# A two-layer perceiver on one core: which engine reads a score's PSUM bank first, and where the second-last chunk's last product and sum stand

## The chip, the cores and the metric

The kernel runs on one core of one Trainium2 chip. The metric is the device time of one execution in microseconds (us); lower is better. Three executions of the kernel before took 2023.55, 2024.21 and 2026.40 us, a median of 2024.21 us.

## The reference

Sixteen batches of 64 latent vectors (width 128) pass through two layers. Each layer has a cross attention to a long context, a sequence model and a feed-forward stage, each added to its input. Cut to what matters here:

```python
x = x + xattn0(ctx, norm(x))          # ctx: 16 batches of 1601 rows of 128
x = x + scan0(norm(x));  x = x + moe0(norm(x))
x = x + xattn1(ctx, norm(x), mask)    # the second layer's scores are masked
x = x + scan1(norm(x));  x = x + ffn1(x)   # ffn1 quantises its inputs to 4 bits

def xattn(ctx, lat):                  # 16 heads of 64
    s = q(lat) @ k(concat(ctx, lat)).T          # + mask
    return softmax(s) @ v(concat(ctx, lat)) @ Wo
```

All arithmetic is in float32 but for a bfloat16 intermediate in the quantiser.

## The kernel before, in words

**Attention groups.** The attention of a layer is cut into 32 groups: 16 batches times two halves of the heads. Both layers make 64 groups. A group takes 13 steps (`NT`); step i works on the i-th 128 rows of the context. The weights are folded in advance, so that a score needs one product of the query side with the transposed context, and the average one product with the context itself.

**A step.** `scores` makes a score tile `s` of 128x512 on TensorE (two matmul records, line 651) in one of three PSUM banks (pool `pss`, 3 buffers). ScalarE copies the tile to SBUF as `st` (line 658; in the second layer line 656, which adds the mask). VectorE keeps a running maximum `R` over the group's tiles, which reads the same bank (line 665, masked 663). The first tile of a group has no maximum, and the second one's reads the first's copy `st`. Once both readers are through, the bank goes to the score three steps on.

**Later steps.** When a group's 13 tiles are done, `maximum` (lines 674 to 685) reduces `R`, `spread` (692) spreads it over the partitions, and `weigh` subtracts it from `st`, two tiles at a time on VectorE (700), followed by the exponential on ScalarE (701). `average` (713) multiplies the weights with the context, 21 steps (`LAG`) behind the score; `gather` (722) takes the sums out of PSUM on VectorE. For the very last group `finish` (737 to 753) does this and normalises and transposes at once; `output` (785) then applies the output weights and adds to the latents `X` (789).

**Work in between.** Loading, normalising and transposing the context, the queries and the second and third parts of each layer are generators. `run` advances them a little after each step under a budget; a generator's `yield` of a tuple puts off its next piece by as many steps (`HOP` is two). For the last part of the second layer the tokens are cut into eight chunks of 128, which are worked off in pairs (0 and 1, 2 and 3, 4 and 5) and then singly (6, 7). Chunk 6's `scan1` and `ffn` are worked off beside the last groups. Chunk 7 holds the last batches and can only begin when the last group is finished: its `scan1` and `ffn` run alone at the end. In `ffn`, line 1393 copies the transposed hidden values `fh`, lines 1398 and 1399 multiply them with the down weights into `fo`, line 1400 adds `fo` to `X` and line 1401 stores the chunk. `layernorm` takes moments (144, 145, 155), a reciprocal root on GpSimd (135) and scales in `scaled` (162). `fill` (128, 130) issues matmuls whose result nobody reads, to keep TensorE running.

**What sets the order.** Each engine works through its own instructions in a fixed order. It is drawn up at compile time: a list scheduler takes, for each engine, the instruction traced earliest of those that are ready by its own estimate of durations. The kernel steers it with edges without a semaphore (`later`, `behind`): `behind` keeps what it traces behind the score evictions that `scores` has listed in `self.place`. Semaphores are added wherever two engines touch the same data or the same PSUM bank.

Of the kernel before, what the change touches and what calls it, by code (L numbers as in the profile page):

```python
# [36 lines left out]
AF = mybir.ActivationFunctionType  # L37
ALU = mybir.AluOpType
# [5 lines left out]
NB, L, D = 16, 64, 128  # L44
# [29 lines left out]
CG = 2  # L74
# [5 lines left out]
class Kernel:  # L80
# [78 lines left out]

    def scaled(self, eng, dst, src, mv, r, n):  # L160
        for c in range(n):
            eng.tensor_scalar(dst[:, c, :], src[:, c, :], mv[:, c, 0:1], r[:, c:c + 1], ALU.subtract, ALU.mult)

    def layernorm(self, dst, src, n, alone=False):

# [472 lines left out]
    def scores(self, g, i):  # L638

        nc, grp = self.nc, self.groups[g]  # L640
        lay, b, half = grp["key"]
        if i == 0:
            grp["st"] = []
            grp["R"] = self.at.tile([P, NQ], F32, tag="R", name=f"R{g}", bufs=2)
        if i % 2 == 0:
            n = min(2, NT - i)
            grp["st"].append(self.at.tile([P, n, NQ], F32, tag=f"st{n}", name=f"st{g}_{i // 2}", bufs=11 if n == 2 else 2))
        st, R = grp["st"][i // 2][:, i % 2, :], grp["R"]
        q = self.q_of[lay, b][:, half * 8:half * 8 + 8, :].rearrange("p h l -> p (h l)")
        s = self.pss.tile([P, NQ], F32, tag="s", name=f"s{g}_{i}")  # L650
        mm = nc.tensor.matmul(s, self.kv_of[lay, b][1][:, i * P:(i + 1) * P], q, start=True, stop=True)  # L651
        self.place["PE"].append(mm.ins)
        masked = lay == 1
        if masked:
            mc = self.mcol[:, i, b:b + 1]
            ev = nc.scalar.activation(st, s, AF.Identity, bias=mc)  # L656
        else:
            ev = nc.scalar.copy(st, s)  # L658
        self.place["ACT"].append(ev.ins)
        if i:  # L660
            last = grp["st"][0][:, 0, :] if i == 1 else R
            if masked:
                mx = nc.vector.scalar_tensor_tensor(R, s, mc, last, ALU.add, ALU.max)  # L663
            else:
                mx = nc.vector.tensor_tensor(R, s, last, ALU.max)  # L665
            self.place["DVE"].append(mx.ins)

    def maximum(self, g):

# [688 lines left out]
    def ffn(self, c0, CG):  # L1358
        nc, tc = self.nc, self.tc
        X = self.X[:, c0:c0 + CG, :]  # L1360
        TG = CG * P
        with tc.tile_pool(name="ff1", bufs=1) as one, tc.tile_pool(name="ff2", bufs=CG) as work:
            t1 = lambda shape, name: one.tile(shape, F32, tag=name, name="ff_" + name)
            xi, xT = t1([P, CG, D], "xi"), t1([P, TG], "xT")
            last = c0 + CG == C and CG == 1
            yield from self.layernorm(xi, X, CG, last)
            flat = xi.rearrange("p c d -> p (c d)")
            yield from self.quant(flat, flat, TG // 16, one, "qx")
            yield HOP
            self.transpose_tokens(xT, xi, CG, f"fft{c0}")  # L1370
            yield HOP
            hb = one.tile([P, CG, I4], F32, tag="hb", name=f"hb{c0}")
            for k in range(CG):
                tg, tu = self.tp(f"fg{k}"), self.tp(f"fu{k}")
                nc.tensor.matmul(tg[:, :I4], xT[:, k * P:(k + 1) * P], self.wgT, start=True, stop=True)  # L1375
                mm = nc.tensor.matmul(tu[:, :I4], xT[:, k * P:(k + 1) * P], self.wuT, start=True, stop=True)
                if c0 + CG == C and CG == 1:
                    self.fill(10, mm)
                sg, th = (work.tile([P, I4], F32, tag=x, name=f"f{x}{k}") for x in ("sg", "th"))
                yield from self.silu2(sg, tg[:, :I4], th)  # L1380
                nc.vector.scalar_tensor_tensor(hb[:, k, :], sg, 0.5, tu[:, :I4], ALU.mult, ALU.mult)
                yield 1.1
            flat = hb.rearrange("p c d -> p (c d)")
            yield from self.quant(flat, flat, CG * I4 // 16, one, "qh", ends=2 if last else 1)
            yield HOP
            hT = []
            for k in range(CG):
                hT.append(work.tile([IC, 512], F32, tag="hT", name=f"fh{c0}{k}"))
                for lo, hi in ((0, 2), (2, 4)) if last else ((0, 4),):
                    t = self.tp(f"ft{c0}{k}")  # L1390
                    for i in range(lo, hi):
                        nc.tensor.transpose(t[:IC, i * P:(i + 1) * P], hb[:, k, i * IC:(i + 1) * IC], self.ident)  # L1392
                    nc.scalar.copy(hT[k][:, lo * P:hi * P], t[:IC, lo * P:hi * P])
                yield 0.1
            yield HOP
            o = self.tp(f"fo{c0}")
            for k in range(CG):
                for i in range(4):
                    nc.tensor.matmul(o[:, k * D:(k + 1) * D], hT[k][:, i * P:(i + 1) * P], self.wdT[:, i, :], start=(i == 0), stop=(i == 3))  # L1399
            nc.vector.tensor_tensor(X, X, o[:, :CG * D].rearrange("p (c d) -> p c d", c=CG), ALU.add)  # L1400
            nc.sync.dma_start(out=self.out.rearrange("(c p) d -> p c d", p=P)[:, c0:c0 + CG, :], in_=X)
            yield 0.5


    def run(self, out):
# [3 lines left out]
        ng = len(self.groups)  # L1409
# [6 lines left out]
        between, prep = [], []  # L1416
# [26 lines left out]
                prep.append((start(lay, b) - 2 if lay or b else 12, 1, self.apart_scores(lay, b)))  # L1443
        prep.sort(key=lambda x: x[0])
        live = []
        n, go, budget, finished = 0, 0, 0.0, 0
        while n < (ng + 1) * NT + LAG + 8 or between:
            for lay in range(2):
                for b in range(NB):
                    if (lay or b > 1) and n == max(start(lay, b) - 48, 8):  # L1450
                        with self.behind():
                            self.context_load(lay, b)
                    if n == start(lay, b) + 14:
                        xeb = self.xeb_of[lay, b] = self.at.tile([P, D + 1], F32, tag="xeb", name=f"xeb{lay}_{b}", bufs=2)
                        self.nc.sync.dma_start(out=xeb, in_=self.xed[lay][b].partition_broadcast(P))
            while prep and prep[0][0] <= n:
                key, _, g = prep.pop(0)

                assert g.__name__ != "latents" or g.gi_frame.f_locals["lay"] == 0 or finished >= 3 + 2 * g.gi_frame.f_locals["gr"]
                live.append([n, g])  # L1460
            for x in list(live):
                if x[0] <= n:
                    try:
                        with self.behind(1):
                            r = next(x[1])
                        x[0] = n + r[0] if isinstance(r, tuple) else n
                    except StopIteration:
                        live.remove(x)
            if n >= 0:
                self.step(n, ng)  # L1470


                hold = ng * NT - 2 <= n < ng * NT + 4
                if n > ng * NT + LAG:
                    stages = [g for _, _, g in between]
                    tails = [chain(*stages[-2:])]
                    if len(stages) > 2:
                        tails.append(chain(*stages[:-2]))
                    while tails:
                        tails = [g for g in tails if self.trace(g, 1)]  # L1480
                    between = []
                if between and between[0][0] <= n:
                    budget = min(budget + between[0][1], 2.0)
                while budget > 0 and not hold and between and between[0][0] <= n and go <= n:
                    try:
                        with self.behind(1):
                            r = next(between[0][2])
                        if isinstance(r, tuple):
                            go = n + r[0]
                        else:  # L1490
                            budget -= r
                    except StopIteration:
                        between.pop(0)
                        finished += 1
            n += 1
# [42 lines left out]
    def step(self, n, ng):  # L1538
        g, i = divmod(n, NT)
# [3 lines left out]
        ga, ia = divmod(n - LAG, NT)  # L1543
        if 0 <= ga < ng and ia:
            if ia == 1:
                self.average(ga, 0)
            self.average(ga, ia)
            if ia == NT - 1:
                (self.finish if ga == ng - 1 else self.gather)(ga)

        for p in (g - 2, g - 1):
            o = n - (p + 1) * NT
# [82 lines left out]
```

## Time and profile before

| what | value |
|---|---|
| three executions, median (lowest to highest) | 2024.21 us (2023.55 to 2026.40) |
| the profiled execution's own time | 2023.47 us |
| its span in the profile | 2021.7 us |
| mean granted TensorE clock | 0.996 |
| busy: TensorE matmul, VectorE, ScalarE, GpSimd | 1974.8, 1563.8, 1382.3, 520.5 us |
| first layer, 0 to 1000 us: busy TensorE, VectorE, ScalarE | 973.99, 760.85, 756.31 us |
| second layer, 1000 to 1960 us: the same | 948.54, 766.88, 609.40 us |
| the end, 1960 to 2022 us: the same | 52.22, 36.03, 16.55 us |

The profile was taken in one execution of its own. Its span is what lies between the first and the last recorded instruction; 1.8 us of its time lie outside. In a row of the groups, the numbers after the first bar are the busy time in us and the mean of one in ns, and after the second bar the engine's idle time just before such an instruction and what ended most of it. In a row of the waits, the numbers are us in total, how often, and the longest. A matmul's end is modelled, so TensorE's busy time holds some waiting too.

### The profile page before, as it was taken

The numbers are of one execution on the slowest core, as the hardware profiler recorded it, in microseconds if no ns is written. First come the engines' busy times: TensorE is split into PE (matmuls) and PEld (weight loads), VectorE is DVE, ScalarE is ACT, GpSimd is POOL, SyncE is SP. The second block draws the span as 40 slices with busy tenths as digits, with TensorE's granted clock in tenths as the row PEclk, the third lists the DMA queues.
The fourth block names the chain that finished last, engine by engine and source line by source line (L and its number), as shares of the span: only waits on it lengthen the run. The fifth ranks groups of instructions, "written<-read, shape, count | busy, mean of one in ns | idle before, by whom it ended". The sixth has DMA issues, their size and how long they took to land. (4 is left out here: it accounts for less than half of the span.)

```text
span 2021.7 us, 32901 instructions
## 1 busy us (share of the span) xinstructions
PE 1974.8 (98%) x12123; PEld 1499.8 (74%) x12123; DVE 1563.8 (77%) x2954; ACT 1382.3 (68%) x2628; POOL 520.5 (26%) x579
## 2 busy tenths in 40 slices
PE   9999999999999989999999999999999999999998
PEld 6777777676777767778777787777778777787787
DVE  6977777886778887676988777898686979778884
ACT  5788878887768887566767657776565656666561
POOL 5111123542123442121543203542111121002000
PEclk9999999999999999999999999999999999999999
DMA  6111112321122321221221102221110110101000
GB/s 175 63 59 46 46 42 84 84 73 50 43 66 84 83 70 36 65 76 45 67 80 51 36 24 72 71 62 51 44 53 18 57 36 22 55 18 36 23 1 22
DMA packets 141805, 110.54 MB, mean 55 GB/s; under 512 B 11458, under 2 KB 127950, under 8 KB 141646
## 3 DMA queue, kind: packets, MB, share of 16 engines
q1 hardware_dynamic: 141102, 108.19, 18.5%
q8 instruction: 96, 1.57, 0.3%
q14 instruction: 63, 0.52, 0.1%
q10 hardware_dynamic: 544, 0.26, 0.0%
HBM read 79.97 MB, written 27.41 MB: 53 GB/s over the span
## 5 line engine op out<-in xcount | busy, mean ns | idle before, releaser
L713 PEld LDWEIGHTS av<-kv,st 128*128 128x128 f32 x6656 | 851.6, 192 | 317.3 <-issue 288.7
L713 PE MATMUL av<-kv,st 128*128 128x129 f32 x6656 | 868.1, 276 | 6.5 <-DVE aq L722 3.9
L651 PE MATMUL s<-qT,kvT 128*128 128x512 f32 x1664 | 853.0, 602 | 17.2 <-DVE R L665 14.2
L700 DVE TENSOR_TENSOR st<-st,mb 128x1024 f32<-128x1024 f32 (+1 forms) x448 | 501.7, 1132 | 1.3 <-PE mb L692 1.1
L701 ACT ACTIVATE st<-st 128x1024 f32<-128x1024 f32 (+1 forms) x448 | 444.9, 997 | 72.1 <-DVE st L700 68.8
L656 ACT ACTIVATE st<-s,mcol 128x512 f32<-128x512 f32 x416 | 283.5, 685 | 221.2 <-PE s L651 178.6
L658 ACT COPY st<-s 128x512 f32<-128x512 f32 x416 | 240.3, 581 | 130.4 <-PE s L651 103.1
L651 PEld LDWEIGHTS s<-qT,kvT 128*128 128x128 f32 x1664 | 259.6, 192 | 84.8 <-DVE R L665 36.1
L663 DVE SCALAR_TENSOR_TENSOR R<-s,mcol,R 128x512 f32<-128x512 f32 x352 | 262.0, 744 | 69.8 <-ACT st L656 68.4
L665 DVE TENSOR_TENSOR R<-s,R 128x512 f32<-128x512 f32 x352 | 240.9, 685 | 90.4 <-ACT st L658 89.3
L762 POOL TENSOR_TENSOR aq<-aq,rd 128x512 f32<-128x512 f32 x63 | 77.6, 1232 | 409.9 <-DVE rd L761 402.6
L565 POOL TENSOR_TENSOR kv<-kv,vec 128x384 f32<-128x384 f32 (+1 forms) x128 | 137.6, 1094 | 151.0 <-PE kt L625 71.7
L866 POOL TENSOR_TENSOR db<-sc_u,bb 128x512 f32<-128x512 f32 x64 | 84.7, 1326 | 134.4 <-DVE h L877 60.8
L883 POOL TENSOR_TENSOR sc_y<-sc_y,h 128x512 f32<-128x512 f32 x60 | 79.9, 1332 | 104.2 <-DVE h L882 80.0
L877 DVE TENSOR_TENSOR_SCAN h<-da,db 128x512 f32<-128x512 f32 x64 | 85.3, 1333 | 0.0
L616 ACT ACTIVATE kv<-kv,coff,crstd 128x128 f32<-128x128 f32 x182 | 76.5, 489 | 5.1 <-POOL coff L613 5.1
L665 DVE TENSOR_TENSOR R<-s,st 128x512 f32<-128x512 f32 x32 | 22.1, 689 | 72.3 <-ACT st L658 72.3
L607 ACT ACTIVATE scr<-kv,cmean 128x128 f32<-128x128 f32 x182 | 72.8, 400 | 6.9 <-DVE cmean L603 3.7
L722 DVE SCALAR_TENSOR_TENSOR aq<-xeb,ee,av 128x129 f32<-128x129 f32 x252 | 72.8, 341 | 1.4 <-PE av L713 1.3
L135 POOL TENSOR_TENSOR crstd<-cvar,neghalf 128x13 f32<-128x13 f32 x14 | 35.0, 2502 | 134.6 <-DVE cvar L611 134.4
L450 PE MATMUL q<-xnT,wqk 128*128 128x128 f32 x512 | 68.8, 277 | 0.0
L450 PEld LDWEIGHTS q<-xnT,wqk 128*128 128x128 f32 x512 | 62.9, 192 | 6.3 <-issue 3.1
(410 smaller groups left out, 1973.5 us busy)
## 6 DMA issues: line engine op xcount, KB each, us to landing
bb<-bcd SPq DMA_DIRECT2D x64, 256.0 KB, 4.4
xh<-kv SPq DMA_DIRECT2D x16, 832.0 KB, 4.8
kv<-xh SPq DMA_DIRECT2D x16, 832.0 KB, 5.5
kvT<-xhT SPq DMA_DIRECT2D x16, 800.0 KB, 4.5
xhT<-kvT SPq DMA_DIRECT2D x15, 800.0 KB, 3.4
kv<-in_ctx_dram SPq DMA_DIRECT2D x15, 768.0 KB, 5.5
ew<-in_e1T_dram SPq DMA_DIRECT2D x36, 64.0 KB, 1.9
ew<-in_e3T_dram SPq DMA_DIRECT2D x36, 64.0 KB, 1.9
```

The source lines that it names most:

```text
L450: nc.tensor.matmul(t[:, k * P:(k + 1) * P], self.wqk[:, g * 4 + k, :], xnT, start=True, stop=True)
L565: nc.gpsimd.tensor_tensor(kv[:, lo:hi, :D], kv[:, lo:hi, :D], self.row(self.vec[:, w1, :], [P, hi - lo, D]), ALU.mult)
L651: mm = nc.tensor.matmul(s, self.kv_of[lay, b][1][:, i * P:(i + 1) * P], q, start=True, stop=True)
L656: ev = nc.scalar.activation(st, s, AF.Identity, bias=mc)
L658: ev = nc.scalar.copy(st, s)
L663: mx = nc.vector.scalar_tensor_tensor(R, s, mc, last, ALU.add, ALU.max)
L665: mx = nc.vector.tensor_tensor(R, s, last, ALU.max)
L700: nc.vector.tensor_tensor(st, st, self.row(mb, [P, n, NQ]), ALU.subtract)
L701: nc.scalar.activation(st, st, AF.Exp)
L713: nc.tensor.matmul(o, st, self.kv_of[lay, b][0][:, i, :], start=(i == 0 and k % 2 == 0), stop=(i == NT - 1 and k % 2 == 1))
L866: nc.gpsimd.tensor_tensor(db, u, self.row(bb[:, 0, s % 2, :], both), ALU.mult)
L877: nc.vector.tensor_tensor_scan(flat(h), flat(da), flat(db), 0.0, ALU.mult, ALU.add)
```

## The change

It has two parts. In `scores`, the running maximum on VectorE is traced ahead of the copy on ScalarE. Both read the same bank, so the semaphore between them turns round: the copy now waits for the maximum of its own tile.

At the end, chunk 6's last product (`fo`) is traced ahead of `finish`: when the last average is traced, `upto_sums` advances the waiting generators until chunk 6's `ffn` has issued it. The sum into `X` (line 1400 before) and the store then come when the generator is next advanced; `later` gives the sum an edge behind the instruction that `scaled` last noted in `self.normed`. Chunk 7's `scan1` is advanced three pieces at once when the tail begins.

```diff
     def scaled(self, eng, dst, src, mv, r, n):
         for c in range(n):
-            eng.tensor_scalar(dst[:, c, :], src[:, c, :], mv[:, c, 0:1], r[:, c:c + 1], ALU.subtract, ALU.mult)
+            self.normed = eng.tensor_scalar(dst[:, c, :], src[:, c, :], mv[:, c, 0:1], r[:, c:c + 1], ALU.subtract, ALU.mult)
...
         masked = lay == 1
-        if masked:
-            mc = self.mcol[:, i, b:b + 1]
-            ev = nc.scalar.activation(st, s, AF.Identity, bias=mc)
-        else:
-            ev = nc.scalar.copy(st, s)
-        self.place["ACT"].append(ev.ins)
+        mc = self.mcol[:, i, b:b + 1] if masked else None
+
         if i:
...
             self.place["DVE"].append(mx.ins)
+        if masked:
+            ev = nc.scalar.activation(st, s, AF.Identity, bias=mc)
+        else:
+            ev = nc.scalar.copy(st, s)
+        self.place["ACT"].append(ev.ins)
...
-            nc.vector.tensor_tensor(X, X, o[:, :CG * D].rearrange("p (c d) -> p c d", c=CG), ALU.add)
+            alone = CG == 1 and not last
+            if alone:
+                self.summed = True
+                yield 0.0
+            x = nc.vector.tensor_tensor(X, X, o[:, :CG * D].rearrange("p (c d) -> p c d", c=CG), ALU.add)
+            if alone:
+                self.later(x, self.normed)
...
+        def upto_sums():
+
+            while not self.summed:
+                with self.behind(1):
+                    if next(between[0][2], None) is None:
+                        between.pop(0)
+
+        self.summed, self.upto_sums = False, upto_sums
...
                         tails.append(chain(*stages[:-2]))
+                    self.trace(tails[0], 3)
                     while tails:
...
             if ia == NT - 1:
-                (self.finish if ga == ng - 1 else self.gather)(ga)
+                if ga == ng - 1:
+                    self.upto_sums()
+                    self.finish(ga)
+                else:
+                    self.gather(ga)
```

## The prediction

> **What bounds the kernel now.** I read the page's busy times and groups first, then the waits by engine, then the timeline around the longest waits and around the end.
>
> ```profile
> PE 1974.8 (98%) x12123; PEld 1499.8 (74%) x12123; DVE 1563.8 (77%) x2954; ACT 1382.3 (68%) x2628; POOL 520.5 (26%) x579
> ...
> L651 PE MATMUL s<-qT,kvT 128*128 128x512 f32 x1664 | 853.0, 602 | 17.2 <-DVE R L665 14.2
> ...
> L658 ACT COPY st<-s 128x512 f32<-128x512 f32 x416 | 240.3, 581 | 130.4 <-PE s L651 103.1
> ...
> L665 DVE TENSOR_TENSOR R<-s,R 128x512 f32<-128x512 f32 x352 | 240.9, 685 | 90.4 <-ACT st L658 89.3
> ```
>
> TensorE is busy 98% of the span: it is the bound, and a change can only win what TensorE waits for. Its scores do wait, and what ends most of that is the running maximum R. The copy takes 581 ns, the maximum 685. The waits give totals:
>
> ```profile
> ACT st L656 <- PE s L651: 178.6, 186, 6.3
> DVE R L665 <- ACT st L658: 161.5, 125, 7.1
> DVE R L663 <- ACT st L656: 121.5, 111, 5.1
> ...
> PE s L651 <- DVE R L665: 14.2, 14, 2.7
> ```
>
> The masked form adds 2.2 us in 4 waits, so TensorE idles 16.4 us in 18 waits for a bank that R has still to release; no other pair of names costs it more than 4. VectorE sits 283 us behind the copies. Nearly all of the 16.4 us fall in the first layer (14.2), where ScalarE is busy 756 of 1000 us; in the second it is busy 609 of 960. Two timelines show the two kinds of bank wait. In the first, ScalarE is late:
>
> ```profile
> 755.40 0.56 ACT L658 COPY st<-s 128x512 f32<-128x512 f32 x1
> ...
> 756.00 0.69 DVE L665 TENSOR_TENSOR R<-s,R 128x512 f32<-128x512 f32 x1 [2.79 <-ACT st L658]
> ...
> 756.74 1.12 PE L651 MATMUL s<-qT,kvT 128*128 128x512 f32 x2 [2.70 <-DVE R L665]
> 756.83 0.57 ACT L658 COPY st<-s 128x512 f32<-128x512 f32 x1
> ...
> 757.74 0.67 DVE L665 TENSOR_TENSOR R<-s,R 128x512 f32<-128x512 f32 x1
> ```
>
> ScalarE was held by a transfer (its scaling of kvT at 752.74 had waited 4.16 us), VectorE stood idle 2.79 us for the copy, and the score followed R's end. In the second kind, VectorE is late:
>
> ```profile
> 356.40 1.05 ACT L658 COPY st<-s 128x512 f32<-128x512 f32 x2
> 356.45 2.34 DVE L700 TENSOR_TENSOR st<-st,mb 128x1024 f32<-128x1024 f32 x2
> ...
> 358.71 0.68 DVE L665 TENSOR_TENSOR R<-s,R 128x512 f32<-128x512 f32 x1
> ...
> 359.45 1.55 PE L651 MATMUL s<-qT,kvT 128*128 128x512 f32 x3 [1.54 <-DVE R L665]
> ```
>
> That R's score had been finished since about 354.4, but its copy only ended at 356.97, so two subtractions (L700, traced later) were put ahead of R. At the end the order is this:
>
> ```profile
> 1979.86 1.06 PE L713 MATMUL av<-kv,st 128*128 128x129 f32 x8
> ...
> 1982.01 0.92 PE L745 MATMUL at<-ident,aq 128*128 128x128 f32 x3 [1.09 <-ACT aq L743]
> ...
> 1986.08 0.54 POOL L135 TENSOR_TENSOR rstd<-var,neghalf 128x1 f32<-128x1 f32 x1 [18.11 <-DVE var L155]
> ...
> 1986.51 1.06 PE L1399 MATMUL fo<-wdT,fh 88*128 88x128 f32 x8
> 1987.60 0.29 DVE L1400 TENSOR_TENSOR X<-X,fo 128x128 f32<-128x128 f32 x1 [1.60 <-PE fo L1399]
> ...
> 1987.81 0.34 DVE L162 TENSOR_SCALAR sd_xi<-X,mv,rstd 128x128 f32<-128x128 f32 x1
> ```
>
> Chunk 7's norm has its reciprocal root at 1986.62 but stands on VectorE behind chunk 6's sum, which waits for chunk 6's product.
>
> **What the skill says.** The Trainium skill, "PSUM — Partial Sum Buffer", section "PSUM bank collisions raise a hardware error": two engines may not touch one bank and quadrant at once, reads against reads included. So one reader must go second whatever the order. The trace agrees: the copy above ends at 755.96 and R starts at 756.00. The same page, "Engine vs sequencer instructions": ScalarE, VectorE and GpSimd queues are strict FIFO. The trace agrees: in the 2.79 us wait, the scan of 1.22 us that ran next stood behind R. "TensorE: Matmul & The Clock Gate", "What's actually happening": the clock halves after an idle window of about 3.4 us. The page grants nine tenths of the clock or more in all slices, and the longest wait for R here is 2.7 us, so I price no clock change.
>
> **Part 1, the maximum first.** Nothing is added or removed: 768 maxima and 832 copies keep their durations. A bank's hold is still its score's end, plus two queue delays, plus 0.58 and 0.69 us. What moves is which delay comes first.
>
> *ScalarE late.* The three maxima can run while ScalarE is held, and the bank is free at the copy's end. In the event at 756 the copies end at 755.96, 757.40 and, for the third (758.10 plus 0.57), 758.67; the R ends were 756.69, 758.41 and 760.13 (759.45 plus 0.68). The releases come 0.73, 1.01 and 1.46 us earlier: 1.4 us won.
>
> *VectorE late with subtractions ahead.* R is ready at its score's end and, traced earlier, goes ahead of the two L700. It would end near 356.45 + 0.68 = 357.1, the copy at 357.7 instead of a release at 359.39: 1.7 us earlier, more than the wait of 1.54. The two L700 come 0.7 us later; their exponentials and averages follow some steps on (LAG is 21 steps, a step some 1.75 us here), which covers it.
>
> *VectorE late with older work ahead.* Here R stays where it is and the copy comes after it: the release is later by a copy, 0.58 to 0.69 us. Behind the waiting copy stand exponentials (L701, 1.0 us), the context's squares and norms (L607, L616) and the scan's exponentials (L865); averages, transposes and GpSimd wait for those. The trace of before doesn't show this wait, so I bound it: nothing if ScalarE has other work queued ahead of the copy, 0.7 us for each of the 18 waits at most, 12.6 us. A gain beyond the first two kinds is not excluded either: the next wait of its kind, TensorE's average on L722 (3.9 us), would follow VectorE being less blocked.
>
> Sum: from 16.4 us, I take half as won by the two favourable kinds (8.2 us) and a third kind in some three places at 0.65 (2 us): 6.2 us net. The half is a choice: both worked examples win half or more, and I did not find the favourable kinds everywhere. What is late next is the copy, on ScalarE.
>
> **Part 2, product and sum.** The product is eight matmul records, 1.06 us. Placed behind the last average it can start at 1980.92, as its input's copy ended at 1980.64, and is through by 1981.98. TensorE idles there until 1982.01 for the first transpose of finish, so it is hidden by 0.03 us; if that cover fails it costs at most 1.06. The sum (0.29) is ready from 1982. By the code it is traced one step after finish and before chunk 7's norm exists, so the edge names chunk 6's own norm, long past: it is not tied behind the last norm. It still fits VectorE's idle stretch ahead of L789 (1983.0 to 1984.98). Put between L741 and L751 it would delay finish by 0.1 to 0.3 us; put behind the variance, the root's 0.66 us would cover it. Chunk 7's norm then starts at 1986.66 instead of 1987.81, the 0.04 us after its root that the later ones show: **1.15 us** won, since everything after hangs on it. The store goes with the sum; on the SP queue stand chunk 7's five loads, and they had waited for the same product (first one at 1987.70), so they come earlier too, and so does GpSimd's memset. The fillers end at 1986.67 and the transpose follows near 1987.1: a gap of half a microsecond.
>
> **Sum.** 6.2 + 1.15 = 7.35 us off the profiled 2023.47 gives 2016.1. The median of the runs is 0.74 above it: **2016.9**.
>
> **The rivals.** (a) *The maximum first wins what it loses*: favourable and unfavourable waits balance, as the hold has the same terms. For it: the sums are symmetric, and VectorE (77%) is no less loaded than ScalarE (68%). Left is part 2: 2023.1. (b) *Slower: ScalarE becomes the blocked engine.* In the first layer it is as busy as VectorE and has the context's norms in its queue; each of the 18 waits grows by 0.6 us, 10.8, less 1.15: 2033.9. For it: FIFO, and releases at group ends stand behind older gathers (L722). It decides once TensorE's waits for copies exceed 16.4 + 1.15 = 17.6 us. Against it: VectorE alone loses 283 us to copies now. (c) *Stronger*: all of 16.4 and the 3.9 behind L722 go: 2002.8. (d) *Part 2 does not do what it says*: the sum elsewhere still costs at most 0.3 us; it moves no case.
>
> **How the numbers follow.** Forecast (2010 to 2020, with (c) its far end) 0.62; (a) 0.15; (b) 0.23. About 0.2% (4 us) is what a measurement of this kernel can tell from no change. Of the forecast 0.02 lies within 4 us, of (a) 0.12, with 0.02 beyond on the fast side and 0.01 on the slow one. Faster 0.62, same 0.14, slower 0.24. The range 2006 to 2031 leaves 0.05 below, in (c), and 0.15 above, the far half of (b).
>
> **What would show it.** Right: TensorE's wait for R gone, its wait for copies under 10 us; VectorE waiting for scores in place of copies; ScalarE waiting for R; in the 756 event, R during ScalarE's hold; in the tail, the product between last average and first transpose and the norm within 0.1 us of its root. Wrong: TensorE's wait for copies over 16 us, or averages waiting for exponentials that stand behind blocked copies.

## The result, and the profile after

The changed kernel takes **2013.77 us** (median of 15 runs, 2010.77 to 2017.36). The kernel before, on the same chip, takes 2021.27 us (15 runs, 2013.49 to 2026.40). The ratio is **0.9966, with a 95% interval of 0.9954 to 0.9977**. The prediction of 2016.9 us stood for a ratio of 2016.9 / 2024.21 = 0.9964. In absolute terms it lies 3.1 us high, since the kernel before has itself a median 2.9 us lower here than in the three runs shown first.

The profiled execution took 2015.88 us, with a span of 2014.2 (before: 2023.47 and 2021.7). The page of the kernel after, first the busy times and then the groups that answer to those shown of before:

```profile
PE 1972.1 (98%) x12123; PEld 1504.3 (75%) x12123; DVE 1559.9 (77%) x2954; ACT 1380.7 (69%) x2628; POOL 516.5 (26%) x579
...
L651 PE MATMUL s<-qT,kvT 128*128 128x512 f32 x1664 | 853.6, 601 | 20.4 <-ACT st L666 11.7
...
L666 ACT COPY st<-s 128x512 f32<-128x512 f32 x416 | 240.6, 580 | 143.9 <-DVE R L661 112.5
L661 DVE TENSOR_TENSOR R<-s,R 128x512 f32<-128x512 f32 x352 | 240.5, 683 | 54.0 <-PE s L651 53.2
```

Lines have moved: the maximum is now line 661 (masked 659), the copy 666 (masked 664), the average 714, the gather 723, the subtraction 701 and the exponential 702. Counts and durations are as before (580 for 581 ns, 683 for 685). The releasers have swapped: VectorE's maximum now waits for the score, ScalarE's copy for the maximum. But the idle time ahead of the scores has not fallen (20.4 us; it was 17.2): it has only another releaser. The waits by engine (engine, operation and line, what it waits for, us in total, times, the longest) give the totals, first TensorE's, then VectorE's and ScalarE's:

```profile
PE s L651 <- ACT st L666: 11.7, 15, 2.3
PE s L651 <- ACT st L664: 8.0, 10, 1.9
...
PE av L714 <- DVE aq L723: 1.6, 5, 0.5
PE mot L177 <- DVE mo_nx L162: 1.5, 2, 1.1
```

```profile
DVE R L661 <- PE s L651: 112.8, 78, 7.9
DVE R L659 <- PE s L651: 80.6, 86, 4.0
```

```profile
ACT st L664 <- DVE R L659: 190.5, 176, 6.5
ACT st L666 <- DVE R L661: 112.5, 105, 4.6
```

TensorE waits 11.7 + 8.0 = **19.7 us** for a score's bank, where it waited 16.4. So the one number that the prediction made its case on went the wrong way, and the time fell all the same. Two lines of before, which the prediction had not shown as lines, show waits that did fall:

```profile
PE av L713 <- DVE aq L722: 3.9, 5, 1.2
PE mot L177 <- DVE mo_nx L162: 2.9, 2, 2.5
```

Averages waiting for a gather went from 3.9 to 1.6 us, a transpose waiting for a norm from 2.9 to 1.5. I added up every wait of TensorE that each profile lists, and the stretches in which the granted clock was half (at half clock, I count half of a stretch as lost; a last stretch in the kernel after, behind TensorE's last matmul, is left out). What is left of the span is nearly a constant, so the difference lies in these accounts:

| us | before | after | difference |
|---|---|---|---|
| wait for a score's bank | 16.4 | 19.7 | +3.3 |
| averages' waits, on all releasers | 6.5 | 2.0 | -4.5 |
| all other waits of TensorE | 20.3 | 16.4 | -3.9 |
| half of the time at half clock (17.1, 13.7) | 8.6 | 6.9 | -1.7 |
| rest of the span | 1969.9 | 1969.2 | -0.7 |
| span | 2021.7 | 2014.2 | -7.5 |

By what TensorE waited for, the 8.4 us of the second and third rows are 5.3 us less for VectorE, 2.3 less for ScalarE (0.9 of them in the tail, where a product now fills a gap), 1.1 less for transfers and 0.3 more for GpSimd.

By place, 6.1 us of the gain lie ahead of layer 1's first score, which starts at 982.6 us before and at 976.5 after. There the waits for a bank *fell* by 2.5 us, the averages' by 1.5, the others by 1.0 and the half clock's cost by 1.7. From that score to the last one the two kernels take 970.1 and 969.8 us: 5.8 us more at the banks, 3.0 less at the averages, 1.7 less elsewhere. The tail gives 1.2.

The two timelines that the prediction worked out went much as it said. ScalarE late, near 756 us (start, duration, engine, line, and in brackets the idle time before and its releaser):

```profile
751.25 0.68 DVE L661 TENSOR_TENSOR R<-s,R 128x512 f32<-128x512 f32 x1
...
752.60 0.94 ACT L634 ACTIVATE kvT<-kvT,vcol 128x768 f32<-128x768 f32 x1 [3.11 <-DMA xhT<-kvT]
...
754.39 0.56 ACT L666 COPY st<-s 128x512 f32<-128x512 f32 x1
...
755.00 1.13 PE L651 MATMUL s<-qT,kvT 128*128 128x512 f32 x2 [0.53 <-ACT st L666]
```

ScalarE is held 3.11 us by the same transfer; a maximum runs in that hold, the bank is free when the copy ends, and TensorE waits 0.53 us where it had waited 2.70. The scores' waits at this place, 2.70, 0.59 and 0.15 us before, are 0.53 and 0.71 now: 2.2 us won where I had worked out 1.4.

VectorE late with subtractions ahead. The score of the prediction's second example now ends at 359.78 us:

```profile
358.76 1.02 PE L651 MATMUL s<-qT,kvT 128*128 128x512 f32 x2
...
361.67 0.68 DVE L661 TENSOR_TENSOR R<-s,R 128x512 f32<-128x512 f32 x1
...
362.26 2.13 PE L651 MATMUL s<-qT,kvT 128*128 128x512 f32 x4
...
362.35 1.21 DVE L701 TENSOR_TENSOR st<-st,mb 128x1024 f32<-128x1024 f32 x1
...
362.65 0.57 ACT L666 COPY st<-s 128x512 f32<-128x512 f32 x1
...
363.27 0.30 PEld L651 LDWEIGHTS s<-qT,kvT 128*128 128x128 f32 x2 [0.81 <-ACT st L666]
```

Two subtractions stood ahead of its maximum before. Now one does, with a scan in front of it, and the next follows the maximum; so the maximum doesn't come straight behind its score, as worked out. It ends at 362.35, the copy at 363.22. So the bank is free 3.4 us after the score's end, where it had been 5.0. The score that takes the bank follows at 363.27, the second of the two in the third line, and TensorE shows no wait ahead of it: the 1.54 us are gone. And the tail:

```profile
1973.49 1.06 PE L714 MATMUL av<-kv,st 128*128 128x129 f32 x8
...
1974.38 1.10 PE L1400 MATMUL fo<-wdT,fh 88*128 88x128 f32 x8
...
1975.64 0.91 PE L746 MATMUL at<-ident,aq 128*128 128x128 f32 x3 [0.16 <-ACT aq L744]
...
1976.57 0.28 DVE L1405 TENSOR_TENSOR X<-X,fo 128x128 f32<-128x128 f32 x1
...
1979.72 0.54 POOL L135 TENSOR_TENSOR rstd<-var,neghalf 128x1 f32<-128x1 f32 x1 [4.01 <-DVE var L155]
...
1980.30 0.34 DVE L162 TENSOR_SCALAR sd_xi<-X,mv,rstd 128x128 f32<-128x128 f32 x1 [0.66 <-POOL rstd L135]
```

The product L1400 fills the gap between the last average and the first transpose, whose start behind the last average hasn't moved (1.09 us after the average's end, before and after). The sum L1405 runs in VectorE's idle stretch, and the norm starts 0.04 us after its root (1979.72 + 0.54 = 1980.26). From the last average's end to the end of the span it is 39.6 us; before it was 40.8.

### The profile page after: what moved, and what is told of

It reads as the page before. It is cut to its first block, busy times and chain, and to the rows that moved or that the text cites. A ratio compares the mean times of both kernels' runs of the same rounds, so it can differ in the third digit from the quotient of the medians.

```text
span 2014.2 us, 32883 instructions
## 1 busy us (share of the span) xinstructions
PE 1972.1 (98%) x12123; PEld 1504.3 (75%) x12123; DVE 1559.9 (77%) x2954; ACT 1380.7 (69%) x2628; POOL 516.5 (26%) x579
## 5 line engine op out<-in xcount | busy, mean ns | idle before, releaser
L651 PE MATMUL s<-qT,kvT 128*128 128x512 f32 x1664 | 853.6, 601 | 20.4 <-ACT st L666 11.7
L565 POOL TENSOR_TENSOR kv<-kv,vec 128x384 f32<-128x384 f32 (+1 forms) x128 | 133.1, 1059 | 176.4 <-PE kt L625 54.1
L763 POOL TENSOR_TENSOR aq<-aq,rd 128x512 f32<-128x512 f32 x63 | 71.4, 1133 | 362.7 <-DVE rd L762 356.6
L884 POOL TENSOR_TENSOR sc_y<-sc_y,h 128x512 f32<-128x512 f32 x60 | 86.0, 1434 | 99.2 <-DVE h L883 82.6
```

The lines of the kernel that those rows point to most:

```text
L565: nc.gpsimd.tensor_tensor(kv[:, lo:hi, :D], kv[:, lo:hi, :D], self.row(self.vec[:, w1, :], [P, hi - lo, D]), ALU.mult)
L884: nc.gpsimd.tensor_tensor(y, y, h, ALU.add)
```

## The experiments

My first theory is the prediction's: a release comes earlier because the maximum no longer stands behind a late copy. The rivals: the hold of a bank doesn't change and something else gains, or the gain lies in the tail, or in what the compile-time order makes of the traced instructions. All ratios are to the kernel before on the same chip, in brackets the 95% interval.

**One part alone.** The tail alone is the kernel before with every line of the diff but the swap in the scores. The maximum first alone is the swap with the tail as it was.

> Part 2 alone: the copy reads first again, chunk 6's product ahead of finish and its sum free of chunk 7's norm. If the norm's late start was all that stood in the tail, the ratio to the kernel before is 0.9994 (1.15 us less), the norm starts within 0.1 us of its root's end, and the time from the last average to the end falls by 1.1 us. If part 2 carries more of the change (its edges move the compile-time order elsewhere), the ratio is nearer to 0.997.

> Part 1 alone: the maximum reads first, the tail as before. The theory that part 1 carries the gain expects a ratio of 0.997 (some 5.7 us less), with the tail's 1.1 us still missing. The rival, that the maximum first wins what it loses and the profiles differ by chance, expects 0.999 to 1.001.

The tail alone gave 0.9996 [0.9983, 1.0008], median 2019.84 us; the maximum first alone 0.9983 [0.9972, 0.9993], 2018.11 us. The tail alone can't be told from nothing by its time, but its profile shows the same 39.6 us from last average to end, and the same 0.04 us between the root's end and the norm:

```profile
1984.10 0.55 POOL L135 TENSOR_TENSOR rstd<-var,neghalf 128x1 f32<-128x1 f32 x1 [4.01 <-DVE var L155]
...
1984.69 0.35 DVE L162 TENSOR_SCALAR sd_xi<-X,mv,rstd 128x128 f32<-128x128 f32 x1 [0.67 <-POOL rstd L135]
```

The waits of TensorE in the kernel with the maximum first alone:

```profile
PE s L651 <- ACT st L666: 12.1, 16, 2.3
PE s L651 <- ACT st L664: 8.0, 10, 1.9
...
PE av L714 <- DVE aq L723: 1.6, 5, 0.5
```

With the tail alone the average's wait for a gather is 3.9 us in 5 as before. So both the longer waits for a bank and the shorter waits of the averages belong to the swap. Part 1 alone won 0.0017, some 3.4 us; the 6.2 us (0.0031) of the prediction lie outside its interval.

**One layer at a time.** Both have the tail; the swap is made in one of the two layers only (`lay == 1` in the second kernel; `copy()` holds the lines that copy a score):

```
+        first = lay == 0
...
+        if not first:
+            copy()
         if i:
...
+        if first:
+            copy()
```

> Part 2, and the maximum first in the first layer only. If the gain comes where ScalarE is the busier engine (first layer), the ratio is that of the whole change, about 0.997. If it comes where VectorE is the busier one (second layer, 767 of 960 us against 612), the ratio is near that of part 2 alone, 0.9994 or above. The profiles after and before differ by 6.1 us at the layers' border and by 0.4 us more at the second layer's last score, which speaks for the first.

> Part 2, and the maximum first in the second layer only. The theory that VectorE is freed of waiting where it is the busier engine expects 0.997 or less here; the theory that the first layer carries the gain expects 0.9994, part 2 alone. If both layers give half, 0.998 here and in the run with the first layer only.

The swap in layer 0 gave 0.9980 [0.9972, 0.9988], 2017.72 us; in layer 1 0.9988 [0.9976, 0.9999], 2018.49 us. Less the tail's 0.0004 that is 0.0016 and 0.0008; with the tail they add up to 0.0028, the whole won 0.0034. Against the tail alone neither gain is clear of the noise by these times, for the intervals overlap; see the granted clock below. The two layers differ in sign by the bank's waits: in the whole change, the unmasked scores of layer 0 wait 11.7 us (before 14.2), the masked ones of layer 1 8.0 (before 2.2). TensorE's waits in layer 1, from 1000 to 1960 us, first of the kernel with the tail alone, then of the one with the swap in layer 1:

```profile
PE av L713 <- DVE aq L722: 3.5, 4, 1.2
PE s L651 <- DVE R L663: 2.2, 4, 0.7
```

```profile
PE s L651 <- ACT st L658: 7.4, 9, 1.9
PE av L718 <- DVE aq L727: 1.3, 2, 1.0
```

In layer 1 the swap costs 5.2 us at the banks, and still the layer takes no longer: 969.0 us from its first score to its last, 970.1 with the tail alone. The averages' waits in all fall from 6.4 us (tail alone) to 5.0 (layer 0) and 4.2 (layer 1), and to 2.0 with both: each layer's swap takes its own share. All waits for VectorE but those for a bank fall from 13.8 to 9.4 us by the swap in layer 1, and not at all (14.0) by the swap in layer 0. So the two layers do not gain in the same way.

**The whole again, and without the first two groups.** In the profile of after, the first of the 40 slices has a granted clock of eight tenths, and one score there waits 2.35 us. The timeline:

```profile
37.24 0.88 ACT L595 ACTIVATE kv<-kv,coff,crstd 128x128 f32<-128x128 f32 x2 [3.25 <-POOL coff L590]
...
38.03 0.56 ACT L666 COPY st<-s 128x512 f32<-128x512 f32 x1
...
38.64 1.13 PE L651 MATMUL s<-qT,kvT 128*128 128x512 f32 x2 [2.35 <-ACT st L666]
```

The copy, now the last reader, stands on ScalarE behind a scaling that waits 3.25 us for GpSimd. Whether this costs time is asked by leaving the copy first in groups 0 and 1:

```
+        first = g >= 2
```

> The whole change once more, beside the next three on one chip: a ratio to the kernel before of 0.9966 as in the first result; 0.998 would say that the parts seen so far (0.9996 for the tail, 0.9983 for the maximum) are all there is.

> The whole change, but the first two groups keep the copy first. In the three profiles that have the maximum first in the first layer, one score near 39 us waits 2.5 us, because its copy stands on ScalarE behind a normalisation that waits for GpSimd, and the granted clock is then halved for 3.4 to 13.7 us. If that is a cost of the order, this run has no such wait and no halved clock near 40 us, and is 2.5 us (the wait) to 7 us (wait and half of the halved time) below the whole change: a ratio to before of 0.993 to 0.9955. If the wait was hidden anyway, the ratio is that of the whole change.

The whole gave 0.9967 [0.9960, 0.9974], 2015.12 us (22 runs). Without the first two groups it gave **0.9951 [0.9939, 0.9964], 2012.22 us** (6 runs), the lowest of all: clearly below the kernel before, and 2.9 us below the whole in the same comparison, though these two intervals overlap a little. The windows of one stretch, 35 to 52 us, of before, after and this one (length, then busy time and instructions of TensorE, its weight loads, VectorE, ScalarE and GpSimd; then the granted clock, the DMA share and GB/s):

```profile
35.00:52.00 17.00, 15.74 (x73) 8.80 (x71) 12.38 (x21) 13.14 (x29) 8.78 (x12) 1.00 0.44 124
```

```profile
35.00:52.00 17.00, 14.65 (x49) 8.65 (x49) 7.35 (x15) 7.24 (x17) 5.90 (x9) 0.70 0.43 121
```

```profile
35.00:52.00 17.00, 15.77 (x77) 9.21 (x76) 12.98 (x23) 13.75 (x29) 8.26 (x11) 1.00 0.43 122
```

In after, TensorE does 49 matmuls where the others do 73 and 77, at a mean clock of 0.70: the wait is followed by 10.2 us at half clock, a cost of 2.35 + 5.1 = 7.5 us at one place. In the whole's own profile only 3.4 us at half clock followed, so there it is 2.35 + 1.7 = 4.0 us, near the 2.9 us that the medians differ by. With the copy first in two groups the wait and the slow clock are gone from this place, and the banks' waits are 16.6 us in place of 19.1. In its one profile other waits, and stretches at half clock further on, took nearly all of that back (span 2011.5, the whole's 2012.0); the gain of 0.0016 rests on the runs, and I read it as likely, not as shown. Either way the profiles show a wait at the start that part 1 brings and the prediction didn't see.

**The maximum from the copy.** To take VectorE out of a bank's hold altogether, the maximum reads the copied score in SBUF (with the tail; copy first; the mask is then in the copy already):

```
-            if masked:
-                mx = nc.vector.scalar_tensor_tensor(R, s, mc, last, ALU.add, ALU.max)
-            else:
-                mx = nc.vector.tensor_tensor(R, s, last, ALU.max)
+            mx = nc.vector.tensor_tensor(R, st, last, ALU.max)
```

> Part 2, and the maximum takes the copied tile st from SBUF in place of the bank (the same values), so that the bank is free at the copy's end while VectorE still stands behind the copies, as before. If the bank's hold is what TensorE pays for, the scores' wait of 23.5 us above mostly goes and the ratio is 0.993 or less. If VectorE's standing behind copies is what costs (gathers, norms), those waits stay, about 10 us for the averages, and the ratio is 0.998 or above.

It gave 1.0220 [1.0204, 1.0236], 2066.83 us: slower by 2.2%, which neither reading had expected. The group of the maximum, from the page, and two lines of its timeline:

```profile
L662 DVE TENSOR_TENSOR R<-st,R 128x512 f32<-128x512 f32 x704 | 545.8, 775 | 146.8 <-ACT st L658 73.6 <-ACT st L656 68.8
```

```profile
708.52 1.27 POOL L880 TENSOR_TENSOR sc_y<-sc_y,h 128x512 f32<-128x512 f32 x1 [2.21 <-DVE h L879]
...
708.78 1.56 DVE L662 TENSOR_TENSOR R<-st,R 128x512 f32<-128x512 f32 x1 [0.40 <-ACT st L658]
```

The maximum's mean went from 685 to 775 ns; beside GpSimd's product of the scan it took 1.56 us. The Trainium skill, "SBUF — State Buffer", section "Who interferes with whom", says that a VectorE instruction with two SBUF inputs contends with a GpSimd instruction that reads SBUF. The trace agrees at this place; the section gives no number for this instruction. VectorE is busy 1628.3 us (before 1563.8), GpSimd 568.8 (520.5). So this run is no clean test of the hold: it shortened the waits for a bank only from 16.4 to 14.1 us and slowed VectorE. What it does show is where TensorE then waits:

```profile
PE av L710 <- DVE aq L719: 17.7, 16, 2.1
PE mb L689 <- DVE tm L680: 9.3, 6, 2.4
...
PE tm L671 <- DVE R L662: 6.9, 6, 3.2
```

With VectorE slower, the averages' wait for a gather grows most, from 3.9 to 17.7 us, besides steps that hang on the maximum's end. All of TensorE's waits for VectorE but those for a bank grow from 14.3 to 51.7 us, while the span grows by 43.7.

**The place in the queue.** Part of the swap's effect might be that a maximum no longer stands behind subtractions that were traced later. In this kernel (with the tail; copy first) each subtraction is kept behind the newest maximum, by an edge of order without a semaphore (`later`):

```
             self.place["DVE"].append(mx.ins)
+            self.newest = mx
...
-        nc.vector.tensor_tensor(st, st, self.row(mb, [P, n, NQ]), ALU.subtract)
+        x = nc.vector.tensor_tensor(st, st, self.row(mb, [P, n, NQ]), ALU.subtract)
+        self.later(x, self.newest)
```

> Part 2 with the copy first, and each subtraction of weigh kept behind the running maximum of its step in VectorE's order (an edge without a semaphore). This removes the subtractions ahead of R (274 of 768 maxima before) without turning the wait round. If it was the place in VectorE's queue that mattered, this gives the gain of the maximum first, 0.998 or less. If it is VectorE's freedom from the copies, VectorE stands behind them more than before and the ratio is 1.000 to 1.004.

It gave 1.0133 [1.0116, 1.0150], 2047.89 us, slower than either reading had expected. VectorE's waits:

```profile
DVE R L665 <- ACT st L658: 170.4, 139, 6.5
DVE R L663 <- ACT st L656: 126.2, 122, 4.7
```

No maximum has a later subtraction ahead of it any more (0 of 768; before 274, after 92), and VectorE stands behind copies 296.6 us instead of 283: the subtractions that used to fill these waits now stand behind them. So moving the maximum ahead gains nothing in this form, as long as it must wait for the copy. It isn't a clean test of the place alone, for the edge also holds back the subtractions, and with them the exponentials and averages. I counted how long VectorE is made to wait: with a score finished and VectorE free, it stood idle ahead of a maximum for 156 us before, 210 here, and **4.7 us after**. ScalarE's idle time of the same kind, ahead of a copy, went the other way, from 65 us to 256.

**What an engine's time is worth.** If moving some 150 us of waiting from VectorE to ScalarE is the gain, then a microsecond of VectorE must be worth more than one of ScalarE. Four kernels add 256 small instructions that are no part of the computation, on one engine or the other, to the tail alone (copy first) or to the whole (maximum first):

```
+        if j % 2 == 0:
+            nc.vector.tensor_tensor(self.spare, self.ident, self.ident, ALU.max)
...
+            nc.scalar.copy(self.spare, self.ident)       # the other two
```

> Part 2 with the copy first, and 256 extra VectorE instructions, four a group (128x128, about 0.29 us each, 74 us in all; their result is not read). It doubles the suspected cost. If TensorE pays for VectorE's time under this order (it is busy and then also stands behind the copies), the time rises by a fair part of the 74 us, 15 us or more (ratio 1.007 and up), and by clearly more than the same load on ScalarE. If VectorE has slack enough, under 4 us (1.002).

> Part 2 with the copy first, and 256 extra ScalarE copies of the same size, four a group (about 0.27 us each, 69 us in all; not read). If VectorE is the engine that limits under this order, this costs less than half of what the extra VectorE work does. If the two are alike, or ScalarE is the limit in the first layer, it costs as much or more.

> The whole change with the same extra VectorE work. If the maximum first frees VectorE of waiting, the load costs less here than with the copy first: its difference to the whole change (0.9967) is smaller than the other's to part 2 alone (0.9996). If the order only moves the waits, the differences are equal within 0.0015.

> The whole change with the same extra ScalarE work. If the maximum first makes ScalarE the blocked engine (it then stands behind R as VectorE stood behind the copies), the load costs more here than with the copy first, and more than the VectorE load does here. If ScalarE has the slack for it, the difference to the whole change is under 0.002.

| added on | copy first, tail alone | maximum first, whole | added by the load |
|---|---|---|---|
| nothing | 0.9996 [0.9983, 1.0008] | 0.9967 [0.9960, 0.9974] | |
| VectorE | 1.0064 [1.0046, 1.0081] | 1.0040 [1.0025, 1.0055] | 0.0068, 0.0073 |
| ScalarE | 1.0020 [1.0012, 1.0029] | 0.9991 [0.9982, 0.9999] | 0.0024, 0.0024 |

The first row is from another chip, each ratio against the kernel before on its own. The load wasn't spread as I had meant: all of it was drawn forward, to between 4 and 335 us on VectorE (84 us of work) and 4 and 292 us on ScalarE (77 us). So these runs speak for the first part of layer 0 alone. There, a load on VectorE costs some 2.8 to 3 times what one on ScalarE costs, in either order. That is against rival (b) in that stretch: ScalarE's load does not cost more with the maximum first. But the theory of a freed VectorE had expected VectorE's load to cost less with the maximum first, and by these ratios (0.0073 against 0.0068) it does not. For layer 1 the runs show nothing.

**The granted clock in the runs.** Every run's result lists its span and its mean granted clock. Much of the noise is the clock: over the 51 runs of the kernel before that stand beside the first four experiments, the span falls by 2.1 us for each 0.001 of clock, near the 2.0 that 0.001 of the span is. With span times (1 - clock) taken off each run, the standard deviation falls from 2.7 to 1.2 us, and the differences of the means to the kernel before become (95% interval in brackets):

| kernel | us less than before | lost to the clock, us (before: 7.9 beside the first four, 8.3 beside the others) |
|---|---|---|
| tail alone | 2.2 (0.8) | 7.8 |
| maximum first alone | 4.2 (0.8) | 8.4 |
| tail, and the swap in layer 0 | 4.4 (0.5) | 8.0 |
| tail, and the swap in layer 1 | 4.6 (0.9) | 9.4 |
| whole | 6.3 (0.7) | 8.0 |
| whole but for groups 0 and 1 | 6.2 (0.9) | 4.4 |

Reckoned so, the parts add up (2.2 + 4.2 = 6.4), each layer's swap gives about 2.3 us on top of the tail, and what groups 0 and 1 gain by the old order is all in the clock. The loads cost 15.9 and 11.8 us on VectorE (copy first, maximum first) and 5.4 and 3.7 on ScalarE, each within 2 us: here VectorE's load is cheaper with the maximum first, as the theory expected. This holds only as far as the time at half clock is chance and not a part of what the load does.

## Why the prediction was right, and which steps of it were not

The sum was right: 0.9964 forecast, 0.9966 measured. It was right by luck in part, for errors cancelled and the largest term failed.

**The failed step: "from 16.4 us, I take half as won".** The wait for a bank was to fall by 6.2 us and rose by 3.3. The two favourable kinds exist (756 and 357 us of before), and in layer 0, where the prediction had found nearly all of the wait, it did fall, but only from 14.2 to 11.7 us. The unfavourable kind was mis-sized: "some three places at 0.65 (2 us)". A place of it in layer 1:

```profile
1140.76 0.74 DVE L659 SCALAR_TENSOR_TENSOR R<-s,mcol,R 128x512 f32<-128x512 f32 x1
...
1140.93 1.06 ACT L702 ACTIVATE st<-st 128x1024 f32<-128x1024 f32 x1 [2.47 <-DVE st L701]
...
1141.89 0.67 ACT L664 ACTIVATE st<-s,mcol 128x512 f32<-128x512 f32 x1
...
1142.62 1.12 PE L651 MATMUL s<-qT,kvT 128*128 128x512 f32 x2 [1.20 <-ACT st L664]
```

The maximum ends at 1141.50. Ahead of the copy on ScalarE stands an exponential that itself waited 2.47 us for a subtraction on VectorE; so the bank is free only at 1142.56, 1.06 us later, and TensorE waits 1.20. In all ten waits for a bank in layer 1 an exponential is the instruction ahead of the late copy. This kind took the waits there from 2.2 to 8.0 us: 5.8, not 2 in all. I had priced the third kind at the copy's own duration, and not at what stands in front of the copy. Counted over all 768 maxima, the time from a score's end to its last reader's end was 2.82 us before and 2.80 after in layer 0, and 2.37 and 2.38 in layer 1. The mean hold is untouched, which is what rival (a) said of it: the two readers have swapped places.

**The term I left as "not excluded" made good the loss.** "The next wait of its kind, TensorE's average on L722 (3.9 us), would follow VectorE being less blocked" stands in the prediction as a possibility and in rival (c). It came: the averages' waits fell by 4.5 us, other waits by 3.9, and 5.3 of these 8.4 us were waits for VectorE. In layer 1 they nearly paid for the banks; in layer 0 they came on top of a smaller wait for a bank. VectorE's 283 us behind copies were the largest number in my waits table. I used them as an argument against rival (b) and gave them no price; ahead of a finished score they were 156 us of blocked queue, with gathers, norms and gate steps in it that TensorE waits for.

**Rival (b), with its deciding point, was crossed and didn't decide.** TensorE's waits for copies are 19.7 us, above the 17.6 from which it was to be slower, and above the 16 that I named as the sign of being wrong. The point was worked out as if nothing else that TensorE waits for could change. In the account above, everything else fell by 8.4 us.

**Part 2: right in each step.** Product hidden, transposes unmoved, norm 0.04 us behind its root, loads and memset earlier; 40.8 to 39.6 us is 1.2, forecast 1.15. Rival (d) was right in that the sum isn't tied behind the last norm: it runs 3.7 us ahead of it, at no cost.

**Two things not priced.** The start: 2.35 us of wait and, in the profiles with the maximum first in layer 0, 3.4 to 13.7 us at half clock; without it (copy first in groups 0 and 1) the ratio is 0.9951. And the clock: from nine tenths or more in all slices I concluded "so I price no clock change", but a stretch of 3.4 us doesn't show in a slice of 50. The kernel before had 17.1 us of them; one, at 759.0, sat right behind the burst whose wait of 2.70 us the swap shortened.

**What stays open.** That VectorE's freed time is the cause of the shorter waits is argued from the counts and in line with the run that slows VectorE (17.7 us at the gathers) and the one that blocks it more (+1.3%). It isn't shown step by step, since the swap also changes the order in which thousands of instructions stand on all engines, and I couldn't hold that order fixed. Where the swap gains is open too: the runs give each layer about the same, the profiles most of it to layer 0. With the cost of half clock taken off, layer 0 lasts 973.8 to 975.8 us in the three of the first eight profiles that keep the copy first there, 971.4 to 972.2 in three that have the maximum first, and 974.1 in the one with the swap in layer 0 alone. Layer 1 lasts 968.4 to 969.3 and 967.3 to 968.2. The account of waits and clock leaves a rest of 1968.4 to 1970.2 us in seven of the eight profiles of before, after and the first six experiments; the one with the swap in layer 0 alone has 4 us more, and the six later experiments have 1971 to 1977, which I can't place.

## What to carry to other kernels

When two engines read one bank in turn, count the mean hold before and after a swap of the two: here it did not change, and what changed is which of the two queues stands still meanwhile. Price the waits behind each queue, not only the wait for the bank, and look at what stands in front of the reader that will now come last. Choose the order by stage: where the other engine's queue has a long wait of its own (here at the start of the first layer), the old order may be the better one. And compare the granted clock of the runs before reading a difference of 0.2%.

## What the runs showed of the hardware that I had not expected

**Short idle times can be followed by half clock.** Windows of the kernel before and after around such stretches (columns as above; the third column from the right is the clock):

```profile
759.00:762.40 3.40, 3.25 (x8) 0.71 (x6) 3.40 (x10) 2.54 (x4) 0.40 (x1) 0.50 0.03 5
```

```profile
39.90:50.10 10.20, 10.20 (x33) 6.67 (x33) 4.95 (x11) 3.82 (x9) 0.42 (x1) 0.50 0.40 112
1244.80:1248.20 3.40, 3.40 (x18) 3.40 (x17) 2.24 (x4) 0.74 (x2) 2.50 (x2) 0.50 0.00 0
```

The clock is 0.50 for 3.4 us or a multiple, 1.3 to 2.3 us after waits of TensorE of 2.70, 2.35 and 1.86 us had ended. The Trainium skill, "TensorE: Matmul & The Clock Gate", section "What's actually happening", puts the window of idleness at about 3.4 us; in these two kernels no single wait is that long, so the measurement decides: waits well under it were followed by half clock. That the waits are the cause isn't shown. Not every wait of this length was followed so (2.23 us at 1713 in the kernel after), and the longest stretch of the kernel before, 6.8 us at 830.7, has no wait of TensorE in the 8 us ahead of it.

**Two SBUF inputs beside GpSimd.** The maximum takes 685 ns with one input in PSUM and 775 ns in the mean with both in SBUF; half of these took 686 ns or less, the longest 1.81 us.
